# A macaron transformer block on one core: weights in quarters, earlier token loads, and reductions per head

## The chip, the cores and the metric

The kernel runs on one NeuronCore of a Trainium2 chip. The engines named here are PE (TensorE, the matmuls), DVE (VectorE), ACT (ScalarE), POOL (GpSimd) and SP (SyncE, which here does nothing but issue DMA transfers). [...] The metric is the device time of one execution, in microseconds. Before the change its median over three runs is 3358.45 us (3357.94 to 3363.19).

## The reference: two feed-forward halves around an attention

The input x has 8 batches of 512 tokens with 512 features, all fp32. Cut to what matters, the reference is:

```python
x = x + 0.5 * ffn(layernorm(x), w_gate, w_up, w_down)
x = x + attention(layernorm(x), W_q, W_k, W_v, W_o)
x = x + 0.5 * ffn(layernorm(x), w_gate, w_up, w_down)
```

- `ffn`: h = silu(x @ w_gate) * (x @ w_up), with 2048 hidden features. Of every four neighbouring hidden features the two of largest magnitude are kept and the others are set to zero. Then h @ w_down gives 512 features again.
- `attention`: 16 query heads and 4 key/value heads of 32 features, rotary positions on queries and keys, a full softmax over the 512 tokens, and an output projection. Head i uses key/value head i modulo 4.
- `layernorm`: no learned scale or shift, epsilon 1e-5.

Both feed-forward halves use the same weights.

## The kernel before, in words

**Blocks and side stages.** There are 16 feed-forward blocks: for each of the 8 batches a first one and a final one. Their order is the list `blocks` (L941): (0,0), (1,0), then (b,0) and (b-2,1) alternating, and last (6,1) and (7,1). The blocks are the main line of the program. Beside them run side stages, written as Python generators: the layer norm of each block, the attention of each batch, and `combine_down`, once. Each `yield` ends one step of a side stage.

**How the order of the instructions is made.** The order is worked out while the program is built, by a small planner. `at` (L125) holds the planned time of PE, DVE and ACT; `takes` (L128) adds a duration. A position n counts groups of matmuls (one is some 3.6 us of planned PE time); a block has WIDTH = 42 positions. A side stage has a first and a last position, and its steps are due in equal paces between them. After every group or half group of the main line, the loop at L1002 looks at each running stage. It takes the next step if that step is due and its data are ready by the plan (`ready <= at["pe"] + TOLD`, L1012), or if it is overdue by more than LATE = 3 positions, ready or not. A stage takes at most one step at each look.

**The order on DVE.** Work for DVE that isn't written at once is put in a queue: `urgent` (through `soon`) or `put_off` (through `later`). `fill` (L331) takes from `urgent` first, then from `put_off`, then the steps of the two-of-four selection (`thin`), as long as the planned DVE time fits under PE's. `ensure` (L155) forces an entry: it runs everything that stands before it in the same queue. `Slots` (L166) does so for a buffer's earlier users before the buffer is taken again.

**The hidden layer.** A block has eight pairs of row groups of gate and up weights. A pair (`woven`, L566) is computed with seven matrix products in place of eight, in the manner of Strassen and Winograd: each takes a quarter of the weights, or a sum of quarters, and a quarter of the transposed tokens, or a sum of those. In order: Q11, S1, S2, S4, S3, Q12, Q22, where S1 = Q21 + Q22, S2 = S1 - Q11, S3 = Q11 - Q21, S4 = Q12 - S2. Each product is eight matmul records of 256 columns (L576). DVE and ACT carry the results through the tiles `row` and `corner`; L588 is the addition on DVE, and L208 and L210 are the copies on ACT or DVE.

**Weights of the hidden layer.** `load_gu` (L90) fills two tiles of four quarters, `w` from the weights and `t` from the sums of quarters kept in DRAM (`gu_sums`). The pool has two buffers of each, so the load for the following pair is issued when a pair begins. In the first block the sums aren't there yet: `w` is loaded in four quarters, `combine_gu` (L636) makes the four sums on DVE in `t`, and after the fourth one DMA writes all of `t` to DRAM. The first pair of that block, and the end of the last block, are computed plainly (`hidden`, L546). `combine_down` (L444) does the like for the down weights during the first block: four chunks of 1 MB, five sums each, put in `put_off`.

**The down projection.** Two chunks of the hidden layer make seven products (`products`, L487; matmuls L506) over sums `e` that POOL makes (L399 to L404), with down weights in three buffers `wd` (L465). They are owed, and are woven into the pairs that follow.

**A layer norm** (`layernorm_t`, L235) issues four token loads of 256 KB (L243), gives way twice, asks DVE for the moments of two token tiles (L249, L250) and then of the other two, has POOL work out scales (L256 to L264), ACT normalise (L267), PE transpose (L223) and ACT copy the result to `xT` (L277). A block's own norm starts 12 positions ahead of it. An attention begins with its weights (three loads, L731), the rotary tables (L735) and then the same norm.

**An attention** (L727) works head group by head group (c, four of them, with four heads each) and token tile by token tile (t, four). `scores` (L788) multiplies queries and keys into `sc`, four banks of 512, and DVE takes the negated maxima (L797) into `nm`, in two reductions over two heads each. `exponentials` (L822) multiplies the transposed scores into `st`, subtracts the maxima through a matmul with ones (L832) and has ACT take the exponential of all four heads into `p` (L835). `weighted` (L840) multiplies `p` with the values, and `summed` (L848) adds the `p` of the token tiles on DVE, in two additions over two heads each. `sc` and `st` share one buffer of four banks; `p` has two buffers. Two steps belong to each (c, t). Operations that go through the queue all carry the line L141 in the profile.

Of the kernel before, what the change touches and what calls it, by code (L numbers as in the profile page):

```python
# [21 lines left out]
SWAP = [i ^ 1 for i in range(32)]  # L22


@with_exitstack
def macaron_block(
# [27 lines left out]
    wgp = ctx.enter_context(tc.tile_pool(name="wgp", bufs=2))  # L54
# [32 lines left out]
    Q11, Q12, Q22, Q21 = range(4)  # L87
    gu_sums = [dram.tile([P, 4, 2, ND // 2, P], FP, name=f"gu_{i}") for i in range(2 * NCH)]

    def load_gu(i, made):  # L90

        w = wgp.tile([P, 4, 2, ND // 2, P], FP, tag="w", name="w")
        t = wgp.tile([P, 4, 2, ND // 2, P], FP, tag="t", name="t")
        if made:
            nc.sync.dma_start(out=w[:, :Q21], in_=w_gu[i // 2, i % 2][:, :Q21])
            nc.sync.dma_start(out=t, in_=gu_sums[i])
        else:
            for q in range(4):
                nc.sync.dma_start(out=w[:, q], in_=w_gu[i // 2, i % 2][:, q])
        return w, t  # L100

    xs = {(0, 0): load_x(0, 0)}
    gu = {(0, 0, 0): load_gu(0, False)}
# [22 lines left out]
    urgent, put_off = deque(), deque()  # L126
# [39 lines left out]
    class Slots:  # L166
# [5 lines left out]
        def tile(self, shape, dtype, name):  # L172
            ensure(self.uses.popleft())
            self.uses.append([])
            return self.pool.tile(shape, dtype, tag=self.tag, name=name)
# [59 lines left out]
    def layernorm_t(got, tag, src=None, xb=None):  # L235
# [54 lines left out]
        if xb is None:  # L290
            yield now
            yield now
# [38 lines left out]
    def fill(slack=HEARD):  # L331

        while True:
            steps = thin["next"]
            for queue in (urgent, put_off):
# [108 lines left out]
    def combine_down():  # L444

        for c in range(NCH):
            raw = p_slots.tile([P, 4, D], FP, "raw")
            nc.sync.dma_start(out=raw, in_=w_down[c])
            yield now
# [9 lines left out]
            for i, name in enumerate(SUMS):  # L459
                made = later(0.7, partial(combine, i, name))  # L460
# [16 lines left out]
    def ffn(b, final, last):  # L477
# [68 lines left out]
        def hidden(h, w, r, cols):  # L546

            n = cols.stop - cols.start
            for m in range(2):
                ps = Bank([P, n], "gu")  # L550
                for k in range(ND):
                    q = ((Q11, Q12), (Q21, Q22))[r % 2][k // 2]
                    nc.tensor.matmul(  # L553
                        out=ps.tile, lhsT=w[:, q, m, k % 2, :], rhs=xT[:, k, cols], start=(k == 0), stop=(k == ND - 1)
                    )
# [10 lines left out]
        def woven(h, w, sums, r, made, last_one):  # L566
# [5 lines left out]
            def product(bank, lhs, rhs, first, ready=0.0):  # L572
# [11 lines left out]
                takes("pe", 1.83)  # L584
                fill()
# [12 lines left out]
            product(x, w[:, Q11], b11, True)  # L598
# [4 lines left out]
            product(v, sums[:, 0], ts[:, 0], True, ensure(made))  # L603
            at_corner = copied(corner, v.tile)
            yield 0.5
            product(x, sums[:, 1], ts[:, 1], False, end)
            end = at_right = copied(right, x.tile)
            yield 0.5
            product(v, sums[:, 3], b22, False, at_corner)
            v.free(end=add(right, v, at_right))  # L610
            yield 0.5
            product(x, sums[:, 2], ts[:, 2], False, end)
# [7 lines left out]
            product(z, w[:, Q12], b21, True)  # L620
# [3 lines left out]
            product(x, w[:, Q22], ts[:, 3], False, end)  # L624
# [11 lines left out]
        def combine_gu(i, w, t):  # L636


            def one(j, a, b, op):
                nc.vector.tensor_tensor(t[:, j], a, b, op)  # L640
                if j == 3:
                    nc.sync.dma_start(out=gu_sums[i], in_=t)

            return [
                later(0.62, partial(one, j, a, b, op))
                for j, a, b, op in (
                    (0, w[:, Q21], w[:, Q22], ALU.add),
                    (1, t[:, 0], w[:, Q11], ALU.subtract),
                    (2, w[:, Q11], w[:, Q21], ALU.subtract),
                    (3, w[:, Q12], t[:, 1], ALU.subtract),  # L650
                )
            ]
# [3 lines left out]
        for c in range(NCH):  # L656
# [19 lines left out]
            if last and c == NCH - 1:  # L676

                ws = [gu.pop((b, final, 2 * c))[0], load_gu(2 * c + 1, False)[0]]
                for half in range(2):
                    for r in range(4):  # L680
                        yield from hidden(h, ws[r // 2], r, slice(half * HALF, (half + 1) * HALF))
# [3 lines left out]
            else:  # L685
                for pair in range(2):
                    i = 2 * c + pair
                    w, sums = gu.pop((b, final, i))
                    ready = gu_made.pop(i, ())

                    following = after(b, final, i)
                    nb, nf, ni = following
                    same = (nb, nf) == (b, final)
                    if not (last and ni == 2 * NCH - 1):
                        gu[following] = load_gu(ni, not (opens and same or last and ni >= 2 * NCH - 2))
                    if opens and i == 0:
                        gu_made[0] = combine_gu(0, w, sums)
                        groups = (g for r in range(2) for g in hidden(h, w, r, slice(0, S)))
                        last_one = gu_made.pop(0)
                    else:  # L700
                        groups = woven(h, w, sums, 2 * pair, ready, last_one)
                    for k, g in enumerate(groups):
                        yield g
                        if k == 3 and opens and same:
                            gu_made[ni] = combine_gu(ni, *gu[following])

                        if pair == 1 and c % 2 == 0 and k in (3, 4):
                            yield from some(1)
                    if i == 2 * NCH - 1:
# [17 lines left out]
    def attention(b):  # L727
# [60 lines left out]
        def scores(c, t, nm):  # L788
# [7 lines left out]
            found = []  # L796
            for two in (slice(0, 2), slice(2, 4)):  # L797
                found.append(soon(
                    1.14, partial(nc.vector.tensor_reduce, nm[:, t, two], sc[:, two, :], AX.X, ALU.max, negate=True)
                ))  # L800
            return [sc_slots.used(found[-1])]
# [20 lines left out]
        def exponentials(c, t, mT):  # L822
# [13 lines left out]
            end = takes("act", 1.88, pe_heard())  # L836
# [237 lines left out]
```

## Time and profile before

| What | Value |
|---|---|
| Median of three runs | 3358.45 us |
| The profiled execution's own time | 3360.9 us |
| Its span, first to last instruction | 3359.1 us |
| Mean granted PE clock | 0.991 |
| PE busy | 3228.8 us, 96% of the span |
| DVE busy | 2256.9 us, 67% |
| ACT busy | 1374.4 us, 41% |
| POOL busy | 573.5 us, 17% |
| Moved by DMA | 463.04 MB, 138 GB/s on average |
| Loads of `t`, 1024 KB each | 118, 7.1 us to landing (median) |
| Loads of `w`, 768 KB each | 118, 4.5 us |
| Loads of tokens for a norm, 256 KB each | 64 from the kernel's own results (6.3 us), 28 from the input (4.6 us) |
| Maxima: reductions of 128x1024 | 256, 1218 ns each |
| Sums of exponentials: additions of 128x1024 | 192, 1250 ns each |
| DVE work of 128x512, such as the copy at L210 | 689 ns each |

The profile is of one execution. A row of the view of waits names who waited, for whom, how long in total, how many times and the longest. A row of the timeline has the start, the duration, the engine, the line and the tiles (out<-in); in brackets stand the idle time of the engine before it and what ended it. "PEld" is the loading of weights into the matmul array, "SPq" SyncE's queue. A busy PE isn't PE at its peak, since the ends of matmuls are modelled; an idle PE is time that no matmul used. The granted clock is the share of full speed that PE was allowed.

### The profile page before, as it was taken

The page shows a single profiled execution, that of the slowest core. Times are in us where ns is not written, and L with a number is a line of the kernel's source. Part 1 is how long each engine was busy: PE and PEld are TensorE (multiplying, and loading weights), DVE is VectorE, ACT ScalarE, POOL GpSimd, SP SyncE. Part 2 cuts the span into 40 slices and gives each one's busy share as a digit, 9 for nine tenths or more (in the row PEclk, how much of TensorE's full clock was granted, in tenths as well). Part 3 has the DMA queues.
Part 4 walks back from the last instruction along what each step waited for, and adds up shares of the span by engine and source line. Part 5 has one row for each costly group of instructions (what it writes and reads, how often), then busy time and mean ns, then how long its engine had stood idle before and what let it go on. Part 6 is the DMA issues. An engine that isn't in the chain of part 4 may idle for free.

```text
span 3359.1 us, 41833 instructions
## 1 busy us (share of the span) xinstructions
PE 3228.8 (96%) x15880; PEld 2328.0 (69%) x15880; DVE 2256.9 (67%) x4491; ACT 1374.4 (41%) x1851; POOL 573.5 (17%) x868
## 2 busy tenths in 40 slices
PE   7999989999999999999999999999999999999999
PEld 5886657766677667766776668765676668665786
DVE  7766865677477765777568765687567765676554
ACT  2222563146424662256314652156425552266221
POOL 1222102201130112111121111211120122200220
PEclk9999999999999999999999999999999999999999
DMA  7553234342433335323433235422532335323451
GB/s 263 181 211 119 73 129 150 129 157 85 157 122 123 144 126 189 109 104 138 170 131 135 98 144 185 147 104 98 185 110 107 132 135 209 120 76 126 148 182 63
DMA packets 160854, 463.04 MB, mean 138 GB/s; under 512 B 14608, under 2 KB 54544, under 8 KB 143760
## 3 DMA queue, kind: packets, MB, share of 16 engines
q1 hardware_dynamic: 160656, 460.38, 38.3%
q8 instruction: 126, 2.06, 0.3%
q14 instruction: 72, 0.59, 0.1%
HBM read 421.53 MB, written 38.80 MB: 137 GB/s over the span
## 4 chain that ended last, share of the span: by engine, by line
PE 84%; DVE 8%; ACT 4%; DMA 3%; issue 1%; SPq 1%; DVEq 0%; ACTq 0%
PE x L576 22%; PE y L506 22%; PE v L576 11%; PE z L576 5%; PE proj L747 4%; PE sc L792 4%; PE ops L843 3%; PE st L827 3%; PE y L921 3%; DMA xn<-x 2%; DVE nm L141 2%; ACT p L835 1%; DVE p L141 1%; PE gu L553 1%; PE tr L223 1%
## 5 line engine op out<-in xcount | busy, mean ns | idle before, releaser
L576 PE MATMUL x<-ts,t 128*128 128x256 f32 x2000 | 483.7, 385 | 7.5 <-DVE row L210 7.5
L506 PE MATMUL y<-wd,h 128*128 128x256 f32 x1984 | 450.8, 381 | 2.9 <-issue 1.1
L576 PEld LDWEIGHTS x<-ts,t 128*128 128x128 f32 x2000 | 373.7, 191 | 115.0 <-issue 41.4
L506 PEld LDWEIGHTS y<-wd,h 128*128 128x128 f32 x1984 | 372.6, 190 | 85.8 <-issue 28.7
L399 POOL TENSOR_TENSOR e<-h 128x512 f32<-128x512 f32 x62 | 90.6, 1461 | 1879.0 <-DVE h L393 1382.2
L215 ACT ACT_TABLE_LOAD x290 | 372.1, 1283 | 5.8 <-PEq L1063 0.7
L141 DVE TENSOR_REDUCE nm<-sc 128x2 f32<-128x1024 f32 x256 | 306.3, 1218 | 86.9 <-PE sc L792 86.2
L506 PE MATMUL y<-wd,e 128*128 128x256 f32 x1488 | 338.9, 382 | 0.2 <-PE den L861 0.2
L506 PEld LDWEIGHTS y<-wd,e 128*128 128x128 f32 x1488 | 280.1, 190 | 65.8 <-issue 22.4
L519 DVE SCALAR_TENSOR_TENSOR x<-y,x 128x512 f32<-128x512 f32 x372 | 242.1, 683 | 123.9 <-PE y L506 121.4
L835 ACT ACTIVATE p<-st 128x2048 f32<-128x2048 f32 x128 | 239.1, 1868 | 144.1 <-PE st L832 105.3
L208 ACT COPY row<-x 128x512 f32<-128x512 f32 x172 | 100.5, 584 | 461.1 <-PE x L576 458.6
L576 PE MATMUL x<-ts,w 128*128 128x256 f32 x1000 | 248.9, 393 | 32.5 <-DVE corner L588 32.5
L576 PE MATMUL x<-xT,w 128*128 128x256 f32 x1000 | 245.9, 390 | 7.5 <-DMA w<-in_w_gu 4.6
L576 PEld LDWEIGHTS x<-ts,w 128*128 128x128 f32 x1000 | 193.1, 196 | 80.6 <-DVE corner L588 35.7
L576 PE MATMUL v<-ts,t 128*128 128x256 f32 x1000 | 240.5, 383 | 6.5 <-DVE t L640 2.5
L141 DVE TENSOR_TENSOR p<-p 128x1024 f32<-128x1024 f32 x192 | 233.8, 1250 | 16.1 <-PE ops L843 14.5
L576 PE MATMUL z<-xT,w 128*128 128x256 f32 x1000 | 240.2, 383 | 2.7 <-issue 1.6
L576 PE MATMUL v<-xT,t 128*128 128x256 f32 x1000 | 241.2, 384 | 0.0
L576 PEld LDWEIGHTS x<-xT,w 128*128 128x128 f32 x1000 | 189.6, 194 | 66.0 <-issue 32.9
L614 ACT ACTIVATE h<-corner 128x256 f32<-128x256 f32 x125 | 51.7, 414 | 430.3 <-DVE corner L588 430.3
L576 PEld LDWEIGHTS z<-xT,w 128*128 128x128 f32 x1000 | 186.8, 190 | 59.0 <-issue 28.0
(112 smaller groups left out, 4522.6 us busy)
## 6 DMA issues: line engine op xcount, KB each, us to landing
t<-gu SPq DMA_DIRECT2D x118, 1024.0 KB, 7.1
w<-in_w_gu SPq DMA_DIRECT2D x118, 768.0 KB, 4.5
wd<-wd SPq DMA_DIRECT2D x155, 512.0 KB, 4.0
wd<-in_w_down SPq DMA_DIRECT2D x124, 256.0 KB, 5.4
x<-x SPq DMA_DIRECT2D x64, 256.0 KB, 2.5
xn<-x SPq DMA_DIRECT2D x64, 256.0 KB, 6.3
w<-in_w_gu SPq DMA_DIRECT2D x40, 256.0 KB, 6.2
x<-in_x SPq DMA_DIRECT2D x32, 256.0 KB, 3.1
```

What stands on the lines that cost most here:

```text
L141: self.does()
L208: nc.scalar.copy(dst, src)
L215: nc.scalar.activation(dummy[:, 1:2], dummy[:, 0:1], f)
L506: nc.tensor.matmul(out=y.tile[:, t, :], lhsT=part[:, t * P : (t + 1) * P], rhs=operands[i][:, n, :], start=(n == 0), stop=(n == 3),)
L519: nc.vector.scalar_tensor_tensor(to, y.tile, 0.5 * sign, to, ALU.mult, ALU.add)
L576: nc.tensor.matmul(out=bank.tile[:, m, :], lhsT=lhs[:, m, k, :], rhs=rhs[:, k, :], start=(first and m == 0 and k == 0), stop=(k == 1), ski ...
L747: nc.tensor.matmul(out=ps.tile, lhsT=wa[:, k, col : col + P], rhs=xT[:, k, :], start=(k == 0), stop=(k == ND - 1))
L792: nc.tensor.matmul(out=sc[:, kv, :], lhsT=qT[rows, c, t * P : (t + 1) * P], rhs=kT[rows, :], start=True, stop=True)
L827: nc.tensor.matmul(out=st[:, kv, :], lhsT=kT[rows, t * P : (t + 1) * P], rhs=qT[rows, c, :], start=True, stop=False)
L835: nc.scalar.activation(p, st, AF.Exp)
L843: nc.tensor.matmul(out=ops[rows, :], lhsT=v[:, t, rows], rhs=p[:, kv, :], start=(t == 0), stop=(t == NT - 1))
L921: nc.tensor.matmul(out=y.tile, lhsT=qT[:, k, t * P : (t + 1) * P], rhs=wo[:, k, :D], start=(k == 0), stop=(k == ND - 1))
```

## The change

1. **Quarters.** The two tiles of four quarters, two buffers each, become sixteen buffers of one quarter (`QUARTERS = 16`): the same space. The list `coming` holds, for all 16 blocks, which quarter of which pair is used in which order. `load_quarters` gives back the buffers of used quarters and loads the next ones. Outside the first block this happens after every product; in the first block after every pair, where S1 to S4 have buffers but no load.
2. **Stores of sums.** `combine_gu` writes each sum to DRAM as it is made, and is called one product earlier (k = 2 for 3).
3. **A third queue.** `for_later` comes after `urgent` and `put_off` and before the selection's steps. The sums of `combine_gu` and `combine_down` go there.
4. **Tokens of a norm.** The two steps that gave way become one that is ready 10 us of planned PE time after the loads. A block's norm starts 15 positions ahead in place of 12, and NORM falls by one. `combine_down` likewise waits 12 us after its load.
5. **Per head.** Maxima and sums of exponentials take four instructions of 512 elements in place of two of 1024.
6. **The planner.** An exponential's planned end counts the wait for its buffer `p`. A step is ready if `ready + TOLD <= at["pe"]`.

```diff
-    wgp = ctx.enter_context(tc.tile_pool(name="wgp", bufs=2))
+    wgp = ctx.enter_context(tc.tile_pool(name="wgp", bufs=QUARTERS))
...
+            if block == blocks[0]:
+                order = Q11, Q12, Q21, Q22, S1, S2, S3, S4
+            elif block == blocks[-1] and i >= 2 * NCH - 2:
+                order = Q11, Q12, Q21, Q22
+            else:
+                order = Q11, S1, S2, S4, S3, Q12, Q22
+            coming.extend((block, i, q) for q in order)
+    quarters = {}
+
+    def load_quarters(*used):
+
+        for key in used:
+            del quarters[key]
+        while coming and len(quarters) < QUARTERS:
+            block, i, q = key = coming.popleft()
+            quarters[key] = w = wgp.tile([P, 2, ND // 2, P], FP, tag="w", name="w")
+            if q <= Q21:
+                nc.sync.dma_start(out=w, in_=w_gu[i // 2, i % 2][:, q])
+            elif block != blocks[0]:
+                nc.sync.dma_start(out=w, in_=gu_sums[i][:, q - S1])
...
         def tile(self, shape, dtype, name):
-            ensure(self.uses.popleft())
+            self.ready = ensure(self.uses.popleft())
...
         if xb is None:
-            yield now
-            yield now
+            there = at["pe"] + 10.0
+            yield lambda: there
...
-            for queue in (urgent, put_off):
+            for queue in (urgent, put_off, for_later):
...
             nc.sync.dma_start(out=raw, in_=w_down[c])
-            yield now
+            there = at["pe"] + 12.0
+            yield lambda: there
             yield now
...
-                made = later(0.7, partial(combine, i, name))
+                made = later(0.7, partial(combine, i, name), at["pe"], for_later)
...
                 takes("pe", 1.83)
+                if not opens:
+                    load_quarters(((b, final), i, q))
                 fill()
...
-                nc.vector.tensor_tensor(t[:, j], a, b, op)
-                if j == 3:
-                    nc.sync.dma_start(out=gu_sums[i], in_=t)
+                nc.vector.tensor_tensor(w[j], a, b, op)
+                nc.sync.dma_start(out=gu_sums[i][:, j - S1], in_=w[j])
...
-                        if k == 3 and opens and same:
-                            gu_made[ni] = combine_gu(ni, *gu[following])
+                        if k == 2 and opens and i + 1 < 2 * NCH:
+                            combine_gu(i + 1)
...
+                    if opens:
+                        load_quarters(*[key for key in quarters if key[:2] == ((b, final), i)])
...
-            found = []
-            for two in (slice(0, 2), slice(2, 4)):
-                found.append(soon(
-                    1.14, partial(nc.vector.tensor_reduce, nm[:, t, two], sc[:, two, :], AX.X, ALU.max, negate=True)
-                ))
-            return [sc_slots.used(found[-1])]
+            for kv in range(N_KV):
+                one = partial(nc.vector.tensor_reduce, nm[:, t, kv : kv + 1], sc[:, kv, :], AX.X, ALU.max, negate=True)
+                found = soon(0.6, one)
+            return [sc_slots.used(found)]
...
-            end = takes("act", 1.88, pe_heard())
+            end = takes("act", 1.88, max(pe_heard(), p_slots.ready + 0.1))
...
-            for two in (slice(0, 2), slice(2, 4)):
-                made = later(1.17, partial(nc.vector.tensor_tensor, p[:, two], p[:, two], before[:, two], ALU.add))
+            for kv in range(N_KV):
+                made = later(0.6, partial(nc.vector.tensor_tensor, p[:, kv], p[:, kv], before[:, kv], ALU.add))
...
-    NORM = 6 + 2 * NT
+    NORM = 5 + 2 * NT
...
-        sides.append((place(b, i) - 12, place(b, i) - 2, NORM, stage, ("attention", b) if i else None, None))
+        sides.append((place(b, i) - 15, place(b, i) - 2, NORM, stage, ("attention", b) if i else None, None))
...
-                if n > side["due"] and ready is not None and (ready <= at["pe"] + TOLD or n > side["due"] + LATE):
+                if n > side["due"] and ready is not None and (ready + TOLD <= at["pe"] or n > side["due"] + LATE):
```

## The prediction

> **What bounds the kernel now.** I read the page's totals first, then the waits of TensorE (PE), then a timeline around the longest of them, then windows with the granted clock.
>
> ```profile
> span 3359.1 us, 41833 instructions
> PE 3228.8 (96%) x15880; PEld 2328.0 (69%) x15880; DVE 2256.9 (67%) x4491; ACT 1374.4 (41%) x1851; POOL 573.5 (17%) x868
> ```
>
> PE is the bound: 3359.1 - 3228.8 = 130.3 us without a matmul, 6.3 of them before the first matmul and 3.7 after the last. The change alters no matmul, so it can win only in the other 120 us and in what they do to the clock. Who owes them (us in total, times, longest):
>
> ```profile
> PE x L576 <- DVE corner L588: 32.5, 8, 7.5
> PE ops L843 <- ACT p L835: 21.1, 19, 2.3
> PE st L827 <- DVE nm L141: 16.3, 36, 2.0
> ...
> PE den L861 <- DVE p L141: 5.5, 5, 1.8
> PE x L576 <- DMA w<-in_w_gu: 4.6, 3, 2.3
> ...
> PE v L576 <- DMA t<-gu: 1.8, 3, 0.7
> ```
>
> The first row names a VectorE (DVE) addition, but the timeline shows that the addition is itself stuck (start, duration):
>
> ```profile
> 585.45 5.80 SPq L243 DMA_DIRECT2D xn<-x  x4
> ...
> 589.07 1.89 PE L576 MATMUL z<-xT,w 128*128 128x256 f32 x8
> 596.88 0.69 DVE L249 BATCH_NORM_STATS2 st<-xn 128x6 f32<-128x512 f32 x1 [8.58 <-DMA xn<-x]
> ...
> 597.71 0.66 DVE L588 TENSOR_TENSOR corner<-x,corner 128x512 f32<-128x512 f32 x1
> ...
> 598.42 2.93 PE L576 MATMUL x<-ts,w 128*128 128x256 f32 x6 [7.46 <-DVE corner L588]
> ```
>
> [...] A norm's moments (L249) stand ahead of the addition and wait 8.58 us for tokens not yet landed; PE then stands 7.46 us. DVE waits this way seven times, 50.4 us in all, at the start of seven of the eight attentions; seven of the eight waits in the first row, 31.9 us, follow from it. The clock suffers too (window, us; the column after POOL is the granted clock):
>
> ```profile
> 586.00:596.00 10.00, 4.96 (x23) 4.01 (x22) 2.31 (x8) 0.98 (x2) 0.00 (x0) 1.00 0.99 349
> 596.00:603.00 7.00, 4.58 (x11) 3.68 (x12) 4.62 (x11) 1.17 (x3) 2.83 (x12) 0.51 0.03 11
> 603.00:613.00 10.00, 10.00 (x48) 8.81 (x47) 8.35 (x22) 3.31 (x6) 7.17 (x16) 1.00 0.51 184
> ```
>
> PE worked at half speed after the stall. The granted mean of 0.991 means 0.009 x 3359 = 30 us lost; taking only what runs after PE has resumed, I count 25 us, of which 13.7 follow six of these seven stalls. The first window also shows why the tokens were late: DMA 0.99 busy.
>
> [...] here SP waits 1231.2 us on PE at L95, the old weight load. [...]
>
> **Part A: tokens of a norm.** Before, the moments came two paced steps after the loads. DVE reached them 4.8 to 7.3 us after SP issued the first attention weight; the first token rows landed 9.8 to 15.6 us after that issue. The step now waits until 10 us of planned PE time have passed, plus 0.15, then for a group boundary and room in the plan: I estimate arrival 3.5 to 4.5 us later than before, 8.5 to 11.5 us. What lands ahead also shrinks: in the example the 1 MB load of t was issued at 581.01, just before the weights at 581.49, and the rows came after 15.4 us; at 913 and 2412, with no such burst ahead, after 9.75 and 9.86 us. Quarters put at most two pieces of 256 KB there. Left over: 0 to 1.5 us of DVE wait, mostly inside the slack of the addition. Worth 31.9 + 13.7 = 45.6 at most; I take **40**. For the other norms the loads move three groups earlier past weight loads on SP; no DVE wait is theirs, so zero. POOL's scale steps move as well, with the sums e (L399 on) queued behind them; POOL is 17% busy and waits there for DVE, also zero.
>
> **Part B: quarters through sixteen buffers.** The bytes are the same (768 + 1024 KB became seven of 256 KB), and so is the space. Issues rise from 2 to 7 per pair: 118 x 5 x about 0.43 us = 254 us more of SP, an otherwise idle engine, cover enough. A product now waits for its own DMA; the old Q11 product did too and all 1000 matmuls of that row idle only 7.5 us, so a landed wait costs about nothing. A quarter is asked for sixteen products ahead instead of seven to fourteen. The three waits on w and three on t (6.4 us, plus 1.7 of clock behind the 2.3 us one) should go: I take **7** of 8.1. The price: SP now follows PE product by product, so loads emitted after a product can no longer leave early. Attention's loads, the output tokens xt (7.0 us to landing, about 10 us ahead) and the wd operands (three buffers, as before) still fit; a cover lost here would be of the order of the old 2 us waits.
>
> **Part C: a queue of its own for weight sums in the first block.** Waits up to 115 us that come of DVE work in bursts or of late weights: 1.4, 2.5, 0.5, 4.8, 1.6, 1.1 and 0.9 us = 12.8, with 3.0 of clock. The worst, 4.8 at 78 us, had five down-weight sums (3.08 us) flushed because an urgent row product stood behind them in one queue. That flush goes. But combine_gu's own four sums are still forced before a pair's second product, now a product earlier, when their weights may just be landing (DVE once waited 5.5 us there). Bounds -3 to +13; I take **8**.
>
> **Part D: per head, and a stricter "ready".** Adding up the PE rows on p, nm, den and transposes in attention gives 56.5 us, with 5.1 of clock. Of the 19 waits on p, nine (10.1 us) come of an exponential that waited for DVE's sums into the same buffer; the plan now counts that. Smaller pieces let a forced flush end after about 0.6 instead of 1.14 us, and steps are taken 0.3 us later in the plan. Estimate: 12 of 21 on p, 7 of 18.7 on nm, 3 of 10.7 on den, none of 6.0 on transposes, which gives **22**. The price: four instructions for two, 128 times for the reduces and 96 times for the additions. [...] where DVE is not held, the trace starts 512-wide instructions 0.60 us apart and the plan's spacing gives 15 and 6. [...] In attention stretches DVE is 0.63 to 0.81 busy (336 to 504 us); I charge **3** on PE's path.
>
> Waits of two blocks on a transposed norm (5 us with clock): **1**. Sum: 40 + 7 + 8 + 22 + 1 - 3 = 75. The profiled execution took 3360.9 us (span 3359.1, 1.8 around it), 2.5 over the median 3358.45; on the median the sum gives 3283.5, so **3284 us**.
>
> **Rivals.**
> *Ten microseconds are too few* (0.20). For it: the rows stand behind 2 MB of attention weights and tables, 9.75 us even uncontended, and SP no longer runs ahead. Then half of A (20), 5 of C, 15 of D, 7, minus 3: 44 won, 3314 us.
> *Attention's waits go as well* (0.13). For it: nine p waits have a named, now planned cause. D 45 in place of 22, and A, B, C almost whole: 108 won, 3250 us. With all 120 us and 25 of clock gone the floor would be 3214.
> *Attention falls behind and is forced* (0.11), the slower one. A step more than LATE = 3 groups overdue is taken whether its data is ready or not. The 10 us wait costs about two groups at once, the stricter test more at each of some 65 steps, and a token of attention needs about 10 us (the exponentials of attention 0 start 11.5 us apart on average). A forced token costs about 2.15 us (the waits of 2.32 and 2.01 us at 432 and 439). A, B and C bring 53 net; beyond 53 / 2.15 = 25 more forced tokens of 128 it is slower, and at 40 it is 3391 us. Against it: the norm's own 13 steps are cheap and can catch up one per boundary, and the last tokens of each attention already run 6 to 10 us apart.
> *The parts cancel, or the streams were hidden anyway* (0.04): 3358 us. For it: B alone is worth only 8. Against: A's waits are plain in the trace.
>
> **Numbers.** Forecast 0.52, its own range 3264 to 3306. A measurement here tells about 0.2%, 7 us. Leaving out the slower case and the best tail, the range is **3247 to 3334**. Faster 0.86 (forecast, the first two rivals, a sliver of the fourth), same 0.03, slower 0.11.
>
> **What would show it.** A right: no row of PE on DVE corner above 3 us, DVE's 50.4 us on xn under 10, granted clock 0.995 or more. B right: no PE wait on a quarter, SP waits spread over all products. C: no wait near 78 us. D: PE's rows on p and nm at half[...]. Wrong: the moments still waiting 4 us or more, or many p and nm waits of about 2 us late in attentions (the forced case), or PE waiting for quarters behind a blocked SP.

## The result, and the profile after

The changed kernel takes 3314.9 us (median; 3314.09 to 3320.04) against 3359.77 us for the kernel before: a ratio of 0.9869, with a 95% interval of 0.9851 to 0.9886. That is 45 us faster. The forecast was 3284, 75 us faster; the range held the result. The profiled execution's span fell from 3359.1 to 3312.3 us, by 46.8.

The page's totals of the kernel after:

```profile
span 3312.3 us, 43741 instructions
PE 3224.5 (97%) x15880; PEld 2322.0 (70%) x15880; DVE 2293.9 (69%) x4949; ACT 1368.8 (41%) x1841; POOL 569.4 (17%) x868
```

PE now stands 87.8 us without a matmul in place of 130.3. The granted clock is 0.994 for 0.991, which is some 10 us less lost to half speed. DVE has 37 us more work. In the rows of waits, `xn` are the token tiles of a norm, `nm` the negated maxima, `p` the exponentials, `den` their sums and `h` the hidden layer. The waits of PE after the change (us in total, times, longest):

```profile
PE ops L854 <- ACT p L846: 18.4, 13, 3.9
PE st L838 <- DVE nm L157: 8.7, 8, 1.5
...
PE x L594 <- ACT row L224: 6.5, 2, 3.2
PE den L872 <- DVE p L157: 6.2, 8, 2.0
PE y L523 <- DVE h L409: 5.7, 2, 3.0
...
PE v L594 <- DVE w L661: 3.7, 1, 3.7
PE x L594 <- DVE corner L608: 3.5, 1, 3.5
```

The first row of before, 32.5 us on the corner addition, is down to one wait of 3.5 us, and that one is in the first block. No PE wait on a weight load is left. But the row on the exponentials `p` has hardly fallen (21.1 to 18.4). A row on ACT's copy of `row` is new, the row on the selection (`h` L409) grew from 0.9 to 5.7 us, and the one on a weight sum (`w` L661) from 2.5 to 3.7. The place shown of before, the start of the second attention, in the timeline of after:

```profile
595.66 0.69 DVE L265 BATCH_NORM_STATS2 st<-xn 128x6 f32<-128x512 f32 x1 [3.92 <-DMA xn<-x]
595.87 1.89 PE L594 MATMUL v<-xT,w 128*128 128x256 f32 x8
...
597.60 3.62 PE L523 MATMUL y<-wd,h 128*128 128x256 f32 x16
```

DVE still waits for the tokens, 3.92 us here, but no matmul waits for DVE. The windows of before, in after:

```profile
586.00:596.00 10.00, 10.00 (x48) 8.81 (x47) 4.32 (x9) 2.49 (x5) 1.27 (x1) 1.00 1.05 363
596.00:603.00 7.00, 7.00 (x35) 6.15 (x34) 6.86 (x22) 1.28 (x2) 4.48 (x14) 1.00 0.99 361
603.00:613.00 10.00, 8.59 (x42) 7.34 (x41) 7.06 (x14) 4.24 (x8) 7.95 (x15) 1.00 0.48 156
```

Through the two stretches in which PE stood 7.46 us and then ran at half speed it is now full, at full clock, with the DMA busy in both (1.05 and 0.99; before, 0.99 and 0.03).

The letters are those of the prediction: A is point 4 of the change, B point 1, C points 2 and 3, D points 5 and 6. By these waits the gain is mainly that of part A. The theory that I put to the test: A brings its whole 45 us, the quarters little; the first block got worse; and in attention a gain was eaten by steps that are forced before they are ready. The rivals: the quarters are what brings the tokens in time; the extra work or the planner's new tests cost what is missing.

### The profile page after: what moved, and what is told of

Read it like the earlier page. It is cut to its first block, busy times and chain, and to the rows that moved or that the text cites. A ratio compares the mean times of both kernels' runs of the same rounds, so it can differ in the third digit from the quotient of the medians.

```text
span 3312.3 us, 43741 instructions
## 1 busy us (share of the span) xinstructions
PE 3224.5 (97%) x15880; PEld 2322.0 (70%) x15880; DVE 2293.9 (69%) x4949; ACT 1368.8 (41%) x1841; POOL 569.4 (17%) x868
## 4 chain that ended last, share of the span: by engine, by line
PE 84%; DVE 8%; ACT 4%; DMA 2%; issue 1%; POOL 1%; SPq 0%; DVEq 0%; ACTq 0%; POOLq 0%
PE x L594 22%; PE y L523 21%; PE v L594 11%; PE z L594 6%; PE proj L760 4%; PE sc L805 4%; PE ops L854 4%; PE st L838 4%; PE y L932 3%; DMA xn<-x 1%; PE tr L239 1%; PE gu L570 1%; ACT p L846 1%; PE den L872 1%; DVE p L157 1%
## 5 line engine op out<-in xcount | busy, mean ns | idle before, releaser
L594 PE MATMUL x<-ts,w 128*128 128x256 f32 x3000 | 726.3, 385 | 12.0 <-ACT row L224 6.5
L594 PEld LDWEIGHTS x<-ts,w 128*128 128x128 f32 x3000 | 562.1, 191 | 170.9 <-issue 55.7
L157 DVE TENSOR_REDUCE nm<-sc 128x1 f32<-128x512 f32 x512 | 321.6, 683 | 87.9 <-PE sc L805 86.6
L846 ACT ACTIVATE p<-st 128x2048 f32<-128x2048 f32 x128 | 238.9, 1867 | 161.8 <-DVE p L157 91.2
L157 DVE TENSOR_TENSOR p<-p 128x512 f32<-128x512 f32 x384 | 254.7, 717 | 6.1 <-PE ops L854 6.0
L594 PE MATMUL v<-ts,w 128*128 128x256 f32 x1000 | 241.2, 384 | 4.3 <-DVE w L661 3.7
L594 PE MATMUL v<-xT,w 128*128 128x256 f32 x1000 | 239.8, 383 | 0.0
L594 PEld LDWEIGHTS v<-ts,w 128*128 128x128 f32 x1000 | 187.9, 191 | 54.4 <-issue 22.4
L594 PEld LDWEIGHTS v<-xT,w 128*128 128x128 f32 x1000 | 186.7, 190 | 51.2 <-issue 12.2
L371 ACT ACTIVATE a<-h 128x1024 f32<-128x1024 f32 x128 | 134.8, 1053 | 204.4 <-DVE m L389 114.0
```

The costliest lines, as they stand in the source:

```text
L157: self.does()
L371: nc.scalar.activation(a, h[:, :, half * HALF : (half + 1) * HALF], AF.Abs)
L594: nc.tensor.matmul(out=bank.tile[:, m, :], lhsT=lhs[:, m, k, :], rhs=rhs[:, k, :], start=(first and m == 0 and k == 0), stop=(k == 1), ski ...
L846: nc.scalar.activation(p, st, AF.Exp)
```

## Experiments: are the tokens the gain, and do they need the quarters?

**Part A alone on the kernel before.**

```diff
+            there = at["pe"] + 10.0
+            yield lambda: there
-            yield now
-            yield now
...
-    NORM = 6 + 2 * NT
+    NORM = 5 + 2 * NT
...
-        sides.append((place(b, i) - 12, place(b, i) - 2, NORM, stage, ...))
+        sides.append((place(b, i) - 15, place(b, i) - 2, NORM, stage, ...))
```

> The kernel before with part A alone: moments 10 us of planned PE time after the token loads, a block's norm 15 positions ahead. If A is the gain by itself: DVE's wait on xn falls from 50 us to under 20, the PE waits on the corner addition at the attentions go, and the time is 3315 to 3325 us (the bursts of 1.8 MB still stand ahead of the tokens, so up to 4 us remain in four attentions). If A needs the quarters to have the tokens landed in time: DVE still waits 30 us or more and the time is above 3338.

Measured: 3331.81 us, ratio 0.9911 (0.9894 to 0.9927), 29 us faster. DVE's wait on xn fell from 50.4 to 8.6 us, and the stalls at the attentions went without any quarters. But the time missed the expected 3315 to 3325. Some waits of the profiled execution, which at 3340.42 us was the longest of the four:

```profile
DVE st L249 <- DMA xn<-x: 8.6, 4, 3.4
PE ops L843 <- ACT p L835: 27.9, 17, 3.6
PE x L576 <- ACT row L208: 6.5, 2, 3.2
```

PE's waits on `p` grew from 21.1 to 27.9 us, and the row on ACT's copy of `row` has come, as in after. Waiting longer has a price, and it lies in attention and in the norms of blocks.

**Tokens ahead of the weights, on the kernel before.** The norm's first step, which issues the four token loads, moves ahead of the weight loads; it waits no longer than before.

```diff
+        norm = layernorm_t(got, "xa", tokens[b][1])
+        first = next(norm)
         for src, col in ((w_k, D), (w_q, 0), (w_v, D + KV)):
             nc.sync.dma_start(...)
...
-        yield from layernorm_t(got, "xa", tokens[b][1])
+        yield first
+        yield from norm
```

> The kernel before, with one edit: an attention issues its four token loads ahead of its weights and tables instead of behind them; no step waits longer. If the seven stalls come of the 2 MB that stand ahead of the tokens: rows land about 5 us after the first issue, DVE's wait on xn is under 10 us, the time 3312 to 3322 us, and no attention is later than before. If the stalls come of a busy DMA in general or of the step being too early in any case: over 3340.

Measured: 3317.6 us, ratio 0.9872 (0.9857 to 0.9887). One reordering of transfers wins about as much as the whole change (43 us for 45). The waits of DVE on the token loads in this kernel:

```profile
DVE st L249 <- DMA xn<-x: 6.6, 7, 2.0
```

50.4 us became 6.6. It isn't quite as expected: in five of the eight attentions DVE still had to wait for the first rows, until 7.0 to 9.0 us after their issue in place of the 5 that I had given them; that was soon enough. PE's waits on `p` stayed at 21.1 and on `nm` at 16.3 us, exactly as before. The stalls came of the 2 MB ahead of the tokens.

**Part A undone in the kernel after.**

```diff
-            there = at["pe"] + 10.0
-            yield lambda: there
+            yield now
+            yield now
...
-    NORM = 5 + 2 * NT
+    NORM = 6 + 2 * NT
...
-        sides.append((place(b, i) - 15, place(b, i) - 2, NORM, stage, ...))
+        sides.append((place(b, i) - 12, place(b, i) - 2, NORM, stage, ...))
```

> The kernel after, with part A undone (two steps that give way, 12 positions ahead). If A is the gain: 3345 to 3360 us, with six or seven PE waits of 2 to 6 us on the corner addition. If the quarters alone thin out what stands ahead of the tokens: 3320 to 3330.

Measured: 3375.49 us, 61 us slower than after and 0.43% (0.29 to 0.58) slower than the kernel before. That is above what I expected. The waits of PE show where:

```profile
PE x L594 <- DVE corner L608: 48.3, 8, 8.8
```

The stalls are longer than in before (48.3 for 32.5 us), and the granted clock is 0.986, so some 47 us are lost to half speed in place of 30. At the second attention DVE reached the moments 4.4 us after SP issued the first attention weight (the start, less DVE's idle time):

```profile
583.54 0.48 SPq L744 DMA_DIRECT2D wqkv<-in_w_k  x1
...
597.20 0.69 DVE L265 BATCH_NORM_STATS2 st<-xn 128x6 f32<-128x512 f32 x1 [9.21 <-DMA xn<-x]
```

In before it was 6.8 us there:

```profile
581.49 0.43 SPq L731 DMA_DIRECT2D wqkv<-in_w_k  x1
```

It is so in all seven attentions that stall: 3.3 to 4.7 us here, 4.8 to 7.4 in before. The first rows came 11.0 to 13.7 us after that issue, for 9.8 to 15.6, so it is not the transfers that are slower: DVE arrives earlier. So quarters alone don't bring the tokens in time. That they make it worse without A, since SP now issues a load after every product and so comes to the attention's loads later, fits these times but isn't shown: this run has the other parts of the change as well.

**The quarters undone in the kernel after.** `load_gu` with two buffers of w and t is back, as in the kernel before, and with it one store of t per pair and `combine_gu` one product later.

```diff
-    wgp = ctx.enter_context(tc.tile_pool(name="wgp", bufs=QUARTERS))
+    wgp = ctx.enter_context(tc.tile_pool(name="wgp", bufs=2))
...
-                if not opens:
-                    load_quarters(((b, final), i, q))
...
-                        if k == 2 and opens and i + 1 < 2 * NCH:
-                            combine_gu(i + 1)
+                        if k == 3 and opens and same:
+                            gu_made[ni] = combine_gu(ni, *gu[following])
```

> The kernel after, with the quarters undone: two buffers each of w and t, loaded pair by pair, one store of t per pair, combine_gu one product later; the rest as after. If the quarters bring what their own waits cost (6.4 us and 1.7 of clock): 5 to 12 us slower than after, 3320 to 3327, with PE waits on w and t back. If they are what lets the tokens land in time: 3335 or more. If they cost in the first block what they bring elsewhere: 3311 to 3318.

Measured: 3311.45 us, ratio 0.9853 (0.9838 to 0.9867), which the intervals can't tell from after. The third reading came, not the first. DVE's wait on the tokens is shorter without quarters than in after:

```profile
DVE st L249 <- DMA xn<-x: 6.3, 4, 2.3
```

In after it is 17.4 us. PE's waits on t are back (2.5 us); in the first block the wait of 3.5 us at 54 us and the one on a weight sum are gone, and one of 4.9 us at 76 us has come. This run mixes the quarters with the first block's calls; the run at the end of the experiments has the quarters alone.

## Experiments: what happened in the first block, and in attention?

**The first block's sums as before.**

```diff
-                        if k == 2 and opens and i + 1 < 2 * NCH:
+                        if k == 3 and opens and i + 1 < 2 * NCH:
...
-                later(0.62, partial(one, j, w[a], w[b], op), at["pe"], for_later)
+                later(0.62, partial(one, j, w[a], w[b], op))
...
-                made = later(0.7, partial(combine, i, name), at["pe"], for_later)
+                made = later(0.7, partial(combine, i, name))
...
-            there = at["pe"] + 12.0
-            yield lambda: there
+            yield now
```

> The kernel after, with the sums of weights in the first block as before: both back in put_off, combine_gu after the fourth product, combine_down giving way twice. If the new queue and the earlier call made the first block worse: the waits up to 120 us fall from 14.7 to about 12 us, with less clock lost, time 3305 to 3311 us. If the new queue helps and only the earlier call costs: 3314 to 3322.

Measured: 3306.51 us, ratio 0.9843 (0.983 to 0.9857): 8.4 us faster than after by the medians, as the theory had it. The intervals just touch (after's begins at 0.9851), though each run of this kernel is faster than each of after. What the new order does is seen in the timeline of after:

```profile
49.94 2.02 DVE L661 TENSOR_TENSOR w<-w 128x512 f32<-128x512 f32 x3 [5.14 <-DMA w<-in_w_gu]
...
53.07 0.68 DVE L608 TENSOR_TENSOR corner<-x,corner 128x512 f32<-128x512 f32 x1
...
53.81 3.78 PE L594 MATMUL x<-ts,w 128*128 128x256 f32 x8 [3.52 <-DVE corner L608]
```

It is the same fault as the tokens' in a new place: a sum called one product earlier meets weights that are still behind a 1 MB chunk of down weights (issued at 39.94, the quarters at 40.45 to 42.19, landed at 47.6 to 49.8), and everything behind it on DVE stands. With the call one product later, as in the run without quarters, this wait is gone. The waits on the selection are another matter: 5.7 us in after, 4.9 in the run without quarters, which keeps the new queue and the longer wait of `combine_down`, and 0.9 here. They go with one of these two, which I didn't part.

**Heads two by two again.**

```diff
-            for kv in range(N_KV):
-                one = partial(nc.vector.tensor_reduce, nm[:, t, kv : kv + 1], sc[:, kv, :], AX.X, ALU.max, negate=True)
-                found = soon(0.6, one)
+            for two in (slice(0, 2), slice(2, 4)):
+                found.append(soon(
+                    1.14, partial(nc.vector.tensor_reduce, nm[:, t, two], sc[:, two, :], AX.X, ALU.max, negate=True)
+                ))
...
-            for kv in range(N_KV):
-                made = later(0.6, partial(nc.vector.tensor_tensor, p[:, kv], p[:, kv], before[:, kv], ALU.add))
+            for two in (slice(0, 2), slice(2, 4)):
+                made = later(1.17, partial(nc.vector.tensor_tensor, p[:, two], p[:, two], before[:, two], ALU.add))
```

> The kernel after, with maxima and sums of exponentials again in two instructions of 1024. If the smaller pieces are what brought the rows on nm down: nm back to 16 us or more, time 3322 to 3332 us. If their use is small: DVE 36 us less busy and the time within 5 us of after, 3310 to 3320. If DVE's extra work is on the path: below 3308.

Measured: 3346.5 us, ratio 0.9958 (0.9946 to 0.9971), 32 us slower than after: the pieces are worth more than I expected of any theory. The profiled execution is the fastest of the five, at 3340.4 us. The waits of PE in it:

```profile
PE ops L856 <- ACT p L848: 22.9, 14, 4.4
PE st L840 <- DVE nm L157: 18.5, 18, 2.0
PE den L874 <- DVE p L157: 9.4, 8, 2.5
```

Against after these are 4.5, 9.8 and 3.2 us more, 17.5 together, and the clock falls to 0.992, another 6 us or so. DVE's 30 us less of work (2263.9 busy) buy nothing. In after a reduction of 512 takes 683 ns and an addition 717 ns. The plan, which reckons with other durations, also forces more steps here (59 for 49, in the table below). How much is due to the length of an instruction and how much to the other order isn't shown.

**The planner's tests undone.**

```diff
-                if n > side["due"] and ready is not None and (ready + TOLD <= at["pe"] or n > side["due"] + LATE):
+                if n > side["due"] and ready is not None and (ready <= at["pe"] + TOLD or n > side["due"] + LATE):
...
-            end = takes("act", 1.88, max(pe_heard(), p_slots.ready + 0.1))
+            end = takes("act", 1.88, pe_heard())
```

> The kernel after, with part 6 undone: a step is ready if its planned time is at most 0.15 us after PE's, and an exponential's planned end doesn't count the wait for its buffer. If counting that wait and the stricter test save the waits that were theirs: rows on p 25 us or more, time 3322 to 3330 us. If they only make attentions later, so that more steps are forced (the planner forces 40 here and 49 in after): 3305 to 3312.

Measured: 3322.77 us, ratio 0.989 (0.9877 to 0.9904), 8 us slower by the medians; the intervals overlap a little (after's ends at 0.9886), so that the tests help is likely rather than shown. And not by the row on p, which is 17.2 us here: `nm` rises from 8.7 to 14.3. The mechanism that I gave was not the one that shows.

**Steps forced later.** One number:

```diff
-    LATE = 3.0
+    LATE = 8.0
```

> The kernel after, with one number changed: a step of a side stage is forced, ready or not, only when it is more than 8 positions overdue in place of 3. The planner then forces 6 steps in all that aren't ready, in place of 49. If the waits of PE in attentions come of forced steps: its rows on p, nm and den fall to half or less and the time is 3285 to 3300 us. If they come of durations that the plan has wrong: 3307 to 3318. If late attentions push their work into the next block's start: above 3320.

Measured: 3258.59 us, ratio 0.9699 (0.9685 to 0.9712), 56 us faster than after and beyond what I expected. The page's window of 100 us in the first attention, after (columns: stretch, us, PE, weight loads, DVE, ACT, POOL, granted clock, DMA share, GB/s):

```profile
420.00:520.00 100.00, 92.10 (x473) 55.06 (x466) 66.56 (x133) 61.27 (x73) 12.07 (x9) 0.98 0.38 122
```

and the same window with 8 positions:

```profile
420.00:520.00 100.00, 98.96 (x546) 66.22 (x544) 74.47 (x158) 64.68 (x81) 12.29 (x10) 1.00 0.41 137
```

PE does 546 matmuls in place of 473 in the same time. The row on p fell from 18.4 to 1.1 us:

```profile
PE ops L854 <- ACT p L846: 1.1, 1, 1.1
```

and the row on `nm` from 8.7 to 0.2. The planner can be made to tell how many steps it took in the main loop while their data were, by its own times, more than 0.15 us from ready. These counts are of the plan, not of the chip:

```
kernel                 steps forced unready
before                          22
tokens_alone                    39
after                           49
tokens_undone                   49
two_heads                       59
planner_undone                  40
late_8                           6
before_late_8                    3
```

The 10 us wait of part A alone takes the count from 22 to 39, which goes with the price that the first experiment met. But it isn't the only cause: without part A the kernel after forces 49 as well. Of the 56 us, 37.7 are PE's idle time (87.8 to 50.1 by the pages) and about 7 the clock (0.994 to 0.996). The remaining 10 lie in PE's busy time, whose ends are modelled; where exactly stays open.

**The same number in the kernel before.**

```diff
-    LATE = 3.0
+    LATE = 8.0
```

> The kernel before, with one number changed: steps are forced at 8 positions overdue in place of 3 (3 steps forced unready in place of 22). If before's waits in attention (some 55 us with the clock) came of forced steps as after's do: rows on p, nm and den at half or less, 3315 to 3335 us, the seven stalls for tokens still there. If they came of what the planner didn't count (the wait for p's buffer, the loose test of ready): above 3345.

Measured: 3331.04 us, ratio 0.9917 (0.9902 to 0.9933), 28 us faster. But the rows didn't halve on nm (16.3 to 10.9) and only nearly on p (21.1 to 11.5): before, forcing was about half of attention's waits. What is left there, 35 short waits of at most 0.6 us on nm, is all but gone in late_8, which has the pieces and the tests as well. I didn't part those two.

## Experiments: a better kernel, and what the quarters are worth

**After with four edits.** Steps forced at 8 positions; an attention's tokens ahead of its weights, as above; 6 us in place of 10 after a norm's loads; the first block's sums as before.

```diff
-    LATE = 3.0
+    LATE = 8.0
...
-            there = at["pe"] + 10.0
+            there = at["pe"] + 6.0
...
+        norm = layernorm_t(got, "xa", tokens[b][1])
+        first = next(norm)
```

> The kernel after with four edits: forced at 8 positions, an attention's tokens ahead of its weights, 6 us in place of 10 after the loads of a norm, and the first block's sums as before the change. If the gains add: 8 us from the first block and 5 to 12 from DVE's 28 us on tokens that the run with 8 positions alone still had: 3238 to 3250. If shorter waits and tokens first bring nothing more: 3250 to 3258.

The first block's edits are those shown above. Measured: 3237.25 us, ratio 0.9636 (0.9622 to 0.965): the best of the study, 78 us faster than after, at the fast end of what I expected if the gains add. PE is busy 3200.1 of 3236.3 us, at a clock of 0.998.

**The first block's sums in queues of their own.** On top of the kernel just shown, in place of its old first block:

```diff
-                later(0.62, partial(one, j, w[a], w[b], op), at["pe"], for_later)
+                later(0.62, partial(one, j, w[a], w[b], op), asked.get(i, 0.0) + 9.0, for_gu)
...
-            for queue in (urgent, put_off, for_later):
+            for queue in (urgent, put_off, for_gu):
...
+                elif for_later and for_later[0].fits(slack):
+                    for_later[0].run()
...
         if (g, name) in combined:
+            ensure(summed_down.pop((g, name), ()))
```

> As the one before, but with the first block's sums in queues of their own: gate and up sums ready only 9 us after their loads, down sums after the selection's steps, and down weights' loads made sure of. If sums that wait for landed weights, and a selection that isn't pushed back, are what the first block lacked: waits up to 120 us below 6 us, and 5 to 12 us faster than the one before. If DVE is simply full there: the same or slower.

Measured: 3244.52 us, ratio 0.9658 (0.9645 to 0.9672), 7 us slower than the one before; the intervals touch, but the slowest run of that one is faster than the fastest of this. But it isn't that DVE is full all along: PE's other waits there are at most 2.4 us. The one, in its timeline:

```profile
107.58 3.10 DVE L479 TENSOR_TENSOR sums<-raw 128x512 f32<-128x512 f32 x5 [8.29 <-DMA wd<-sums]
...
112.58 2.04 PE L602 MATMUL z<-xT,w 128*128 128x256 f32 x4 [9.15 <-issue]
```

The down sums, put last, were forced at the end ten at a time. The second five wait 8.29 us for the stores of the first five to free their buffer, and PE stands 9.15 us at the same place; the profile names nothing that ended this wait. Neither reading that I had written down holds.

**The quarters alone undone, in the best kernel.** Two buffers of w and t again, all else, and the planner's times, as in late_8_tokens_first.

```diff
-    wgp = ctx.enter_context(tc.tile_pool(name="wgp", bufs=QUARTERS))
+    wgp = ctx.enter_context(tc.tile_pool(name="wgp", bufs=2))
...
-                if not opens:
-                    load_quarters(((b, final), i, q))
```

> As late_8_tokens_first, but with the weights of the hidden layer in two buffers of w and t, loaded pair by pair and stored as one t: the quarters alone are undone, the planner's times are the same. If the quarters save only the waits on w and t that before had: 3 to 9 us slower, 3240 to 3247 us, and a few PE waits on w and t. If their issues or the queue that follows PE cost as much: within 3 us of 3237. If they are the reason why tokens land in time: DVE's wait on xn above 30 us and the time above 3255.

Measured: 3245.33 us, ratio 0.9655 (0.9642 to 0.9668), 8 us slower by the medians (7 when each is set against its own runs of before); the two intervals still touch. The waits of PE that come back are the ones that before had:

```profile
PE v L576 <- DMA t<-gu: 3.8, 6, 0.9
PE x L576 <- DMA w<-in_w_gu: 2.6, 3, 1.4
```

6.4 us, as in before. DVE's wait on xn is 4.2 us without the quarters and 12.3 with them: they don't bring the tokens in time here either.

## Why the prediction was right, and where its sum was wrong

The sign, the cause of the largest term and the range were right. The forecast's own range, 3264 to 3306, was missed; the stated one held because it left room for the rivals. By terms, read from the two profiled executions, with the half-speed stretches behind a wait counted at half their length:

| Term | Predicted | Measured |
|---|---|---|
| A, tokens | 40 of 45.6 | 45.6: all seven waits and the slow stretches behind them went |
| B, quarters | 7 of 8.1 | 8.1 by the waits that went; alone, in the best kernel, 7 to 8, with intervals that touch |
| C, first block | +8 | -7 (waits 12.8 to 14.7 us, slow stretches 3.0 to 7.8); undoing it won 8.4 |
| D, attention, with DVE's price | 22 - 3 | 7 (waits 56.5 to 46.3 us, slow stretches 5.1 to 7.8) |
| Norms of blocks | +1 | -3 |

The terms add up to 51, which is 4 more than the 46.8 measured; other small waits that came aren't assigned. The 28 us by which the forecast was too high are mainly C (15), D (12) and the norms (4); A and B brought 7 more than was taken.

**A** was right in its mechanism and nearly in its size. DVE reached the moments 9.1 to 10.8 us after the first issue, as estimated. One step failed without harm: that little more than two quarters would stand ahead of the tokens, so that DVE waits 1.5 us at most. The rows came 10.8 to 14.1 us after the first issue (at the second attention, for one, down weights had been issued just ahead as well, at 579.2 to 581.6 us). DVE still waits 17.4 us in all and 4.5 at the longest, and a wait of 4 us or more was among my signs of being wrong. The slack of the corner addition, which I had only assumed, covers it: no matmul waited. That part is luck. The rival *ten microseconds are too few* names nearly the measured time (3314). The rows were late, as it said, but the half of A that it took off for that wasn't lost.

**B** was right in its mechanism: the 6.4 us of waits and the 1.7 of clock went, and the waits come back when the quarters alone are undone. Its price, that SP follows PE product by product (in after it waits for PE 280 times, 813.6 us in all, on the products x at L116 alone), I called a cover that holds. With A it does. Without A all other parts together make the kernel 15 us slower than before (3375.49 for 3360.84), where with A they make it 17 us faster (3331.81 to 3314.9); the earlier arrival of DVE at the tokens speaks for B as the reason, but the parts weren't separated there.

**C** failed at the step that took +8 between its bounds of -3 and +13; even the bounds were missed. I had named the danger, sums one product earlier meeting weights that have just landed, and DVE's earlier wait of 5.5 us there, but didn't price the stall that such a wait hands to PE, nor the half clock behind it. The flush of 4.8 us went, as predicted; waits of 3.5 us on the addition, 3.7 on a sum and twice about 3 on the selection came. That the selection pays for the new queue or for the later down sums isn't in the prediction at all.

**D** failed at its net, and at the row on `p`. I took 12 of 21 us there, since the plan now counts an exponential's wait for its buffer; 2.7 went, undoing that count left the row at 17.2, and ACT's own wait for DVE's additions into `p` grew from 38.4 us (19 times) to 91.2 (31 times). Undone one at a time, D's parts are worth 32 us (pieces) and about 8 us (tests), more than the 22 that I gave them together. What took some of the gain away is the term that I had set against a rival, *attention falls behind and is forced*: the 10 us wait makes steps late (39 forced with it alone), and so do the other parts (49 without it). I gave it as an all-or-nothing case with 25 further forced tokens as its turning point. The plan forces 27 further steps, of every kind and not only the two of each token, and the loss sits inside the result: LATE = 8 brings 56 us in after. Since it brings 28 in before too, about half of that is, by this comparison, a loss that the change added. It belonged in the sum as a cost, not only among the rivals. My argument that the norm's cheap steps would catch up was wrong.

**Norms of blocks.** At two blocks' norms ACT waits for POOL's scales, and a copy of `row` behind it holds PE 3.2 us. The first of them (`rs` are the scales):

```profile
556.46 0.81 ACT L283 ACTIVATE xn<-xn,rs 128x512 f32<-128x512 f32 x1 [4.74 <-POOL rs L280]
...
557.17 0.56 ACT L224 COPY row<-x 128x512 f32<-128x512 f32 x1
...
557.79 2.75 PE L594 MATMUL x<-ts,w 128*128 128x256 f32 x6 [3.24 <-ACT row L224]
```

In after the plan forces three steps of such norms, in before none. I had called POOL's moved scale steps free.

DVE is busy 2293.9 us, 37 more than before, with 683 ns for a reduction of 512 and 717 ns for an addition. The plan's spacing had given 15 and 6, 21 together. The 3 us on PE's path were my estimate: with heads two by two DVE has 30 us less work and the kernel is 32 us slower, so a cost of it on PE's path isn't shown.

## What to carry to other kernels

In before the corner addition of the second attention had its operand from PE at 589.23 us (a product that started at 587.34 and took 1.89) and started at 597.71, behind moments that had waited 8.58 us for tokens. When an engine stands before a load like this, with other work behind, look first at what was issued ahead of that load: putting the small urgent transfer ahead of the large ones won here about as much as a change with six parts, and lengthened no wait in attention. If instead a step is made to wait, follow the deadline that it is now late for; a rule that takes an overdue step whether or not it is ready turns that lateness back into stalls. Weigh a stall of some microseconds with the half-speed stretch behind it: here it cost 0.43 of the stall again for the seven stalls at the tokens (13.7 for 31.9 us) and 0.53 in the first block of after (7.8 for 14.7), but only 0.17 for attention's shorter waits in after (7.8 for 46.3).

## What the runs showed that I had not expected

Raising the planner's limit from 3 to 8 positions won 56 us in after and 28 in before, without a change to any operation. Splitting reductions of 1218 ns into pieces of 683 ns, and the additions likewise, costs DVE 30 us of work and yet, undone, made the kernel 32 us slower, with DVE nowhere above 0.9 busy in a slice of the page. And the clock made stalls count more than their length in these runs. A stall needn't be long for that: in before, a wait of 2.32 us that ended at 431.7 us was followed by 3.4 us at half speed (a granted clock of 0.50). What brings the half speed on isn't shown. Part A undone has no more PE gaps between its first and last matmul than the kernel before (119.2 for 120.2 us), yet is 15 us slower, at a granted clock of 0.986 for 0.991.
